# Idle transposes on TensorE in the first and in the last group of an RWKV-6 block

## The chip, the core and the metric

One core of a Trainium2 chip runs the whole kernel. The metric is the device time of one execution in microseconds (us), the median of the runs; everything is in 32-bit floats. The engines are named as in the profile: PE is TensorE (matmuls; PEld is its loading of weights), DVE is VectorE, ACT is ScalarE, POOL is GpSimd, and SP issues most of the DMA transfers.

## The reference

An RWKV-6 block: time mixing with a recurrence per head, then channel mixing. x is 32 sequences of 128 tokens and 512 channels, in 32 heads of 16.

```python
xn = ln(x);  sx = token_shift(xn, state)
xxx = tanh((xn + sx * maa_x) @ maa_w1)              # 5 x 32 columns
x5  = xn + sx * (maa_stack + xxx @ maa_w2)          # five mixed inputs
w = exp(-exp(time_decay + tanh(x5[1] @ decay_w1) @ decay_w2))
r, k, v, g = x5[3] @ Wr.T, x5[0] @ Wk.T, x5[2] @ Wv.T, silu(x5[4] @ Wg.T)
for t in range(128):                                # per head, state s is 16 x 16
    a = k_t[:, None] * v_t[None, :]
    out_t = r_t @ (u * a + s);  s = a + w_t[:, None] * s
att = groupnorm(out) * gn_w + gn_b
x = x + (att * g) @ Wo.T
xn2 = ln(x);  sx2 = token_shift(xn2, state)
rr = sigmoid((xn2 + sx2 * maa_r) @ ffn_Wr.T)
kk = relu((xn2 + sx2 * maa_k) @ ffn_Wk.T) ** 2
x = x + rr * (kk @ ffn_Wv.T)
```

## The kernel before

**Tiles and groups.** The 32 sequences are taken in 8 groups of 4. A group's activations are held channel by token: 4 blocks of 128 channels (index e) by 512 columns (4 sequences of 128 tokens). In the recurrence the 128 partitions are the 4 x 32 heads of a group.

**The streams of a group.** Each is a generator that yields its steps:

- front_mix (L422): loads x (L286); layernorm (L319): statistics on DVE (L332, L333: one pair per sequence), rstd on DVE and POOL (L350, and the power in L352), the negated mean in L354 on DVE, the normalization on ACT (L357), transposes on PE (L377, 16 per group), scale and bias on ACT (L367). Then the token shift and the first mix (L433 to L438), the matmuls with maa_w1 (L444 and, in first_split, L397), tanh, and the mix proper: matmuls L410, and per block two DVE steps (L470, L472), or from group 1 on, for three of the five inputs, DVE L465 and POOL L467. In group 0 it also calls constants() (L247), which issues the loads of the small vectors and weights and makes four small POOL products of vec (L249 to L252).
- front_proj (L492): the decay and the projections k, r and v (L391), evicted by ACT (L540) and sent through DMA to the layout of the recurrence. front_gate (L546) does the gate, which waits in DRAM.
- prep (L567): states, products of pairs and the bonus.
- the recurrence (rec_*, L670 to L776): ACT L679 and L690, POOL L704 (am) and L708 (a), DVE the scan L726 and the product L728, PE the sums L761 (transposes that accumulate), ACT the copy L775 of the sums to y. The sums lie in "acc", a PSUM tile of two banks of which there is one buffer.
- back (L784): group normalization (ACT L803 squares; DVE L806, then a Newton iteration L809 to L816, then L818), transposes L829, ACT L838, DVE L840 with the gate from a DMA (L833), matmuls with Wo L849, residual L858, the second layernorm (L357, L377, L367 again), DVE L872 and L884 and POOL for the two mixed inputs, matmuls L391 (fk), L923 (fr), L939 (fv), the output L928 and L930, and its DMA L932. For the last group, back runs as two streams of two sequences each: last1 and last2.
- center (L296) takes the mean over each head out of the weights wv, on POOL (L303 to L310), and stores them in DRAM.

**What sets the order.** Nothing runs as the generators are written down: a planner (class Plan, L73 to L179) records every step once, in one order, and the engines' queues then run it. A step names its engine, an estimate of its time, what it reads and writes, what buffers it takes and frees. The planner keeps estimated times at which each engine is free, looks at each stream's next step, and takes, among those that could start within EPSILON of the earliest, the one with the least due value (L177). DUE (L49) gives each stream its due values at its first and last step, counted in groups. So a change of EPSILON, of DUE or of a stream can move steps of others on every engine, and with them the DMAs on SP's queue.

[...] PSUM is divided by L221 into four one-bank tiles "ps" for matmul results, two "sc" for the scan and the two banks of "acc".

```python
        (ps, [P, N], "ps", 4), (ps, [P, DH, T2], "sc", 2), (ps, [P, DH, P], "acc", 1),
```

The line numbers here are those of the kernel before. In the changed one they are one higher from L239 to L946, and 15 higher in the lines that add the streams to the plan.

Of the kernel before, what the change touches and what calls it, by code (L numbers as in the profile page):

```python
# [8 lines left out]
F32 = mybir.dt.float32  # L9
# [5 lines left out]
P = 128  # L15
# [5 lines left out]
NG = B // GB  # L21
# [14 lines left out]
PE, DVE, ACT, POOL, SP = range(5)  # L36
# [6 lines left out]
LANDING = 2.0  # L43
HOP = (0.2, 0.05, 0.05, 0.04, 0.08)
ON_POOL = (2, 3, 4)
EPSILON = 0.0388


DUE = {"rec": (0.171, 1.108), "mix": (-4.67, -2.417), "proj": (-4.683, 4.311), "gate": (0.588, 0.608), "prep": (-4.19, 1.684), "back": (-0.012, 3.928), "last1": (-21.388, 9.796), "last2": (10.392, 13.665)}  # L49


class Buf:
# [20 lines left out]
class Plan:  # L73
# [103 lines left out]
    def pick(self, best):  # L177
        t0 = min(t for t, _ in best)
        return min((x for x in best if x[0] <= t0 + EPSILON), key=lambda x: x[1][3] + x[1][4] * x[1][2])  # L179


@with_exitstack
def rwkv6_block(ctx: ExitStack, tc: tile.TileContext, x, prev, s0, vecs, u, maa_w1, maa_w2,
# [11 lines left out]
    nc = tc.nc  # L195
    ctx.enter_context(tc.manual_schedule())
    const = ctx.enter_context(tc.tile_pool(name="const", bufs=1))
# [5 lines left out]
    def tag(pool, shape, name, bufs):  # L203
        def make():
            count[0] += 1
            return pool.tile(shape, F32, tag=name, bufs=bufs, name=f"{name}_{count[0]}")
        return make, bufs
# [14 lines left out]
    plan = Plan({name: tag(pool, shape, name, bufs) for pool, shape, name, bufs in spec})  # L222
# [12 lines left out]
    dw2p = const.tile([P, E // 2], F32, name="dw2p")  # L235
    thb = Buf(const.tile([P, N], F32, name="thb"))
    ident = const.tile([P, P], F32, name="ident")
    mhalf = const.tile([P, GB], F32, name="mhalf")
    by_head = const.tile([P, P], F32, name="by_head")  # L239
    make_identity(nc, ident)  # L240
# [543 lines left out]
    def back(g, d, bs=range(GB), W=None):  # L784
# [158 lines left out]
        if W is None:  # L943
            frt.open = fvt.open = False

    data = [dict() for _ in range(NG)]  # L946
    for gen, n in ((rec_dve, 2), (rec_pool, 3), (rec_act, 1), (rec_state, 1), (rec_pe, 2), (rec_out, 0.1)):
        v0, v1 = DUE["rec"]
        plan.add(gen(range(NG)), v0, NG - 1 + v1, n * NU * NG)
    for g in range(NG):  # L950
        for gen, name, n in ((front_mix, "mix", 40), (front_proj, "proj", 72), (front_gate, "gate", 17),
                             (prep, "prep", 40), (back, "back", 140)):
            v0, v1 = DUE[name]
            if name != "back" or g < NG - 1:
# [4 lines left out]
    for bs, name in (((0, 1), "last1"), ((2, 3), "last2")):  # L959
        v0, v1 = DUE[name]  # L960
        plan.add(back(NG - 1, data[-1], bs, W), NG - 1 + v0, NG - 1 + v1, 130)
    plan.run()


# [35 lines left out]
```

## Time and profile before

| | |
|---|---|
| median of 3 runs | 1533.85 us (1533.52 to 1534.64) |
| profiled execution, its own time | 1535.0 us |
| span of its instructions | 1533.2 us |
| mean granted TensorE clock | 0.959 |
| busy: PE / PEld / DVE / ACT / POOL | 1410.0 / 746.6 / 1270.9 / 656.2 / 1024.8 us |
| instructions | 16578 |
| period of a steady group | 170.26 us |
| DMA, mean over the span | 96 GB/s |

A view of instructions has, per row: start and duration in us, the engine, the line, the operation, output <- input by the program's names, the size of the stationary operand, the shape, the type and the count (x) of instructions that the row joins; in brackets, the idle time before it on its engine and what ended it. A matmul of 512 columns in 32-bit floats counts as two in the profile, a transpose as one. "PEclk", and "granted clock" in a table by stretch, is the clock that TensorE was allowed, as a share of full speed; in this trace it is 0.5 or 1.0 at any one moment. Busy tenths divide the span into 40 equal slices of 38.3 us.

### The profile page before, as it was taken

What the parts mean: (1) busy time and instruction counts of PE and PEld (TensorE: products, weight loads), DVE (VectorE), ACT (ScalarE), POOL (GpSimd) and SP (SyncE); (2) the same over time, 40 slices, a digit from 0 to 9 for tenths busy, and PEclk for the clock granted to TensorE, in tenths of its full rate; (3) what the DMA queues carried; (4) which work ended last, traced back from release to release, by engine and by line L of the source; (5) the groups of instructions that cost most, each with busy time, mean ns of one, the idle gap of its engine ahead of it and who ended that gap; (6) DMA issues with size and microseconds to landing.
All of it is one profiled execution on the core that took longest, in us unless ns stands there. A gap on an engine that the chain in (4) does not pass through costs nothing.

```text
span 1533.2 us, 16578 instructions
## 1 busy us (share of the span) xinstructions
PE 1410.0 (92%) x5344; PEld 746.6 (49%) x5344; DVE 1270.9 (83%) x1618; ACT 656.2 (43%) x1277; POOL 1024.8 (67%) x632
## 2 busy tenths in 40 slices
PE   3997898899999999999999999999999998778788
PEld 1343454455554555455554555455544555455444
DVE  5537789989998899899988899899988898878732
ACT  4233242423743356323743365424733354344242
POOL 3014893877787859687786959686777959678400
PEclk9798899899999999999999999999999999889879
DMA  6120331244304431244304521343305421400220
GB/s 223 42 84 23 104 108 29 78 132 145 117 11 144 144 131 43 79 133 142 117 29 134 183 92 35 97 140 124 110 32 163 126 89 41 159 27 28 93 71 28
DMA packets 127559, 146.88 MB, mean 96 GB/s; under 512 B 8176, under 2 KB 77296, under 8 KB 126448
## 3 DMA queue, kind: packets, MB, share of 16 engines
q1 hardware_dynamic: 92112, 128.81, 25.6%
q10 hardware_dynamic: 35360, 17.02, 3.9%
q8 instruction: 42, 0.69, 0.2%
q14 instruction: 45, 0.37, 0.1%
HBM read 94.41 MB, written 17.83 MB: 73 GB/s over the span
## 4 chain that ended last, share of the span: by engine, by line
PE 51%; DVE 27%; POOL 13%; issue 6%; DMA 2%; ACT 1%; SPq 1%; DVEq 0%; POOLq 0%; ACTq 0%
PE ps L391 18%; PE acc L761 8%; POOL am L704 7%; PE ps L939 6%; PE ps L923 6%; PE ps L410 6%; DVE sc L726 5%; POOL a L708 4%; DVE rm L728 4%; PE ps L849 2%; DVE rk L642 2%; DVE ps L634 2%; PE ps L397 2%; PE ps L444 2%; DVE ps L470 1%
## 5 line engine op out<-in xcount | busy, mean ns | idle before, releaser
L704 POOL TENSOR_TENSOR am<-v,k 128x1024 f32<-128x1024 f32 x256 | 610.3, 2384 | 88.7 <-DMA r<-blk 70.4
L391 PE MATMUL ps<-mx,wt 128*128 128x512 f32 (+1 forms) x1312 | 583.2, 593 | 8.8 <-DVE mx L472 3.4
L708 POOL TENSOR_TENSOR a<-am 128x504 f32<-128x504 f32 x256 | 286.1, 1118 | 201.5 <-DVE sc L726 181.1
L391 PEld LDWEIGHTS ps<-mx,wt 128*128 128x128 f32 x1312 | 244.3, 194 | 276.2 <-issue 259.1
L728 DVE TENSOR_TENSOR rm<-sc,r 128x1024 f32<-128x1024 f32 x256 | 312.9, 1222 | 38.3 <-PE acc L761 22.9
L726 DVE TENSOR_TENSOR_SCAN sc<-sc,a 128x512 f32<-128x512 f32 x256 | 313.4, 1224 | 32.7 <-POOL a L708 30.5
L761 PE MATMUL acc<-by_head,rm 128*128 128x128 f32 x2176 | 290.8, 283 | 36.0 <-DVE rm L728 29.9
L761 PEld LDWEIGHTS acc<-by_head,rm 128*128 128x128 f32 x2176 | 252.3, 146 | 135.9 <-issue 54.4
L679 ACT COPY sc<-w 128x512 f32<-128x512 f32 x256 | 151.4, 591 | 219.5 <-DVE rm L728 197.0
L690 ACT COPY a<-st 128x8 f32<-128x8 f32 x256 | 52.2, 204 | 180.1 <-DVE sc L726 156.4
L467 POOL TENSOR_TENSOR mx<-mx,xnT 128x512 f32<-128x512 f32 x84 | 99.7, 1198 | 40.9 <-DVE mx L465 40.3
L923 PE MATMUL ps<-wt,mx 128*128 128x512 f32 x256 | 115.7, 595 | 0.0
L540 ACT COPY blk<-ps 128x512 f32<-128x512 f32 x96 | 56.0, 584 | 137.6 <-PE ps L391 137.6
L849 PE MATMUL ps<-wt,mx 128*128 128x512 f32 x256 | 112.8, 598 | 0.6 <-DVE rk L642 0.6
L410 PE MATMUL ps<-tha,w2p 64*128 64x512 f32 x256 | 89.1, 677 | 18.0 <-DVE mx L472 12.0
L939 PE MATMUL ps<-wt,ev 128*128 128x512 f32 x224 | 102.4, 600 | 2.7 <-DVE mx L472 2.7
L352 POOL TENSOR_TENSOR rstd<-rstd,mhalf 128x4 f32<-128x4 f32 (+1 forms) x17 | 20.2, 1191 | 120.1 <-DVE rstd L350 120.1
L470 DVE SCALAR_TENSOR_TENSOR ps<-ps,vec,sx 128x512 f32<-128x512 f32 x76 | 57.3, 753 | 36.7 <-PE ps L410 36.3
L465 DVE SCALAR_TENSOR_TENSOR mx<-ps,vec,sx 128x512 f32<-128x512 f32 x84 | 61.8, 743 | 21.8 <-PE ps L410 21.7
L849 PEld LDWEIGHTS ps<-wt,mx 128*128 128x128 f32 x256 | 48.9, 192 | 62.5 <-issue 56.5
L923 PEld LDWEIGHTS ps<-wt,mx 128*128 128x128 f32 x256 | 46.4, 190 | 51.0 <-issue 46.8
L939 PEld LDWEIGHTS ps<-wt,ev 128*128 128x128 f32 x224 | 40.9, 192 | 45.3 <-issue 39.9
(108 smaller groups left out, 1341.1 us busy)
## 6 DMA issues: line engine op xcount, KB each, us to landing
x<-in_x SPq DMA_DIRECT2D x15, 1024.0 KB
wt<-in_wk SPq DMA_DIRECT2D x8, 1024.0 KB
wt<-in_wr SPq DMA_DIRECT2D x8, 1024.0 KB
wt<-in_wg SPq DMA_DIRECT2D x8, 1024.0 KB
dgate<-blk SPq DMA_DIRECT2D x32, 256.0 KB
wt<-in_wo SPq DMA_DIRECT2D x8, 1024.0 KB
wt<-in_fk SPq DMA_DIRECT2D x8, 1024.0 KB
wt<-in_fr SPq DMA_DIRECT2D x8, 1024.0 KB
```

The costliest lines, as they stand in the source:

```text
L391: nc.tensor.matmul(p, lhsT=w[:, c, e * P : (e + 1) * P], rhs=xin[:, c, cols], start=(c == 0), stop=(c == NE - 1))
L410: nc.tensor.matmul(p.t, lhsT=w[h, :], rhs=t[h, :], start=True, stop=True)
L467: nc.gpsimd.tensor_tensor(bt(x5[:, f, :]), bt(x5[:, f, :]), row(xnT, f, 1), ALU.add)
L679: nc.scalar.copy(sc.t, d["w01"][:, q : q + 1, :].to_broadcast([P, DH, T2]))
L704: nc.gpsimd.tensor_tensor(am.t, v[:, ds, :], k[:, q : q + 1, :].to_broadcast([P, DH, L]), ALU.mult)
L708: nc.gpsimd.tensor_tensor(a[:, :, 1:T2], am2[:, :, 0 : T2 - 1, 0], am2[:, :, 0 : T2 - 1, 1], ALU.add)
L726: nc.vector.tensor_tensor_scan(scf, scf, a.t.rearrange("p d n -> p (d n)"), 0.0, ALU.mult, ALU.add)
L728: nc.vector.tensor_tensor(pair(rm.t), sc.t.unsqueeze(3).to_broadcast([P, DH, T2, 2]), r2[:, q : q + 1, :, :].to_broadcast([P, DH, T2, 2]), ...
L761: nc.tensor.matmul(acc[:, i, :], lhsT=rm[:, i, :], rhs=by_head, is_transpose=True, start=(q == 0 and i % 4 == 0), stop=(q == S), skip_grou ...
L849: nc.tensor.matmul(p.t, lhsT=att[:, c, b * L : (b + 1) * L], rhs=wot[:, c, :], start=(c == 0), stop=(c == NE - 1))
L923: nc.tensor.matmul(p.t, lhsT=xr[:, c, b * L : (b + 1) * L], rhs=frt[:, c, :], start=(c == 0), stop=(c == NE - 1))
L939: nc.tensor.matmul(p2.t, lhsT=kv[:, c, b * L : (b + 1) * L], rhs=fvt[:, c, :], start=(c == 0), stop=(c == NE - 1))
```

## The change

Two streams are added, each of one generator, `warm(n, need)`: n steps of two transposes of the identity matrix into the banks of acc, and at the end a copy by ACT of one column to a new tile thw of one column, which nothing reads. The results of the transposes are used nowhere. "warm0" has 90 steps (180 transposes), is free to begin at once, and has due values around those of group 0's front; "warm1" has 60 steps (120 transposes), begins after the last sums have been copied (`"rec" in data[NG - 1]`), and is due among the last group's back. EPSILON goes from 0.0388 to 0.0457, and the due values of the other streams are set anew, last2's by the most.

```diff
-EPSILON = 0.0388
+EPSILON = 0.0457
-DUE = {"rec": (0.171, 1.108), "mix": (-4.67, -2.417), "proj": (-4.683, 4.311), "gate": (0.588, 0.608), "prep": (-4.19, 1.684), "back": (-0.012, 3.928), "last1": (-21.388, 9.796), "last2": (10.392, 13.665)}
+DUE = {"rec": (0.169, 1.075), "mix": (-5.141, -3.246), "proj": (-5.191, 5.259), "gate": (0.565, 0.599), "prep": (-4.508, 1.678), "back": (0.059, 3.118), "last1": (-21.936, 10.98), "warm0": (-5.0, -3.0), "warm1": (5.624, 7.819), "last2": (6.858, 12.052)}
...
+    thw = Buf(const.tile([P, 1], F32, name="thw"))
...
+    def warm(n, need):
+        acc = None
+        for _ in range(n):
+            if acc is None:
+                (acc,) = yield Op(PE, 0.215, w=[(0, None)], alloc=["acc"], need=need)
+            else:
+                yield Op(PE, 0.215, w=[(acc, None)])
+            for i in range(2):
+                nc.tensor.transpose(acc[:, i, :], ident, ident)
+        yield Op(ACT, 0.2, r=[(acc, None)], w=[(thw, None)], end=[acc])
+        nc.scalar.copy(thw[:, 0:1], acc[:, 0, 0:1])
...
+    for name, n, need in (("warm0", 90, None), ("warm1", 60, lambda: "rec" in data[NG - 1])):
+        v0, v1 = DUE[name]
+        plan.add(warm(n, need), (0 if name == "warm0" else NG - 1) + v0, (0 if name == "warm0" else NG - 1) + v1, n)
```

What the planner makes of it, by the two orders of instructions:

- PE, front: 110 of the 180 transposes stand before the first L377, 18, 8 and 28 behind its second, third and fourth group of four, 16 between L397 and the first L410.
- PE, end: 50 of the 120 stand behind the last L761 and before the first L829; 36 behind the first two pairs of L829; 8 among the next; then come the eight matmuls of L849 for the first half (16 in the profile's count), 8, a pair of L829, 8, a pair of L829, 10, and L849 of the second half, with four transposes L377 of the first half between its two sequences.
- SP, front: the load of wv (1 MB), which stood second, right behind x, now stands behind all constants and before wk; vec and pv follow x at once.
- DVE, front: four pairs of statistics (group 1) stand before the mix of group 0 instead of eight (groups 1 and 2); the other four are spread over the mix.
- The steady groups keep their order but for one L391 ahead of one L761, one L728 behind the first L872, and a few steps of ACT. Some more steps change places in groups 0 and 1 (130 to 340 us) and in 1290 to 1445 us.
- SP, end: the load of x for the first half and the gates of the halves come in another order.

## The prediction

> **What bounds the kernel now.** I read the page first, then the busy time in nine stretches of 170 us, then the instructions in the first 70 us and in the last 90. On the page, the busy tenths in 40 slices show where TensorE (PE) isn't full, and the clock row where it is slow; the chain says who sets the end.
>
> ```profile
> PE   3997898899999999999999999999999998778788
> ...
> PEclk9798899899999999999999999999999999889879
> ...
> PE 51%; DVE 27%; POOL 13%; issue 6%; DMA 2%; ACT 1%; SPq 1%; DVEq 0%; POOLq 0%; ACTq 0%
> ```
>
> A full clock is 9 or more in that row. It dips in the first slices and in the last seven or so; between them PE is full and the clock too. The table by stretch says the same in numbers (first, a middle, the last; columns: stretch, its length, then PE, weight loads, DVE, ACT, POOL busy, granted clock, DMA share, GB/s):
>
> ```profile
> 0.00:170.00 170.00, 123.44 (x353) 53.66 (x354) 99.89 (x151) 59.51 (x105) 49.77 (x43) 0.87 0.28 88
> 681.20:851.50 170.30, 167.89 (x666) 88.74 (x665) 156.18 (x198) 80.33 (x156) 130.02 (x79) 1.00 0.33 106
> 1362.00:1533.00 171.00, 138.21 (x499) 80.46 (x497) 97.97 (x142) 70.68 (x144) 67.72 (x42) 0.88 0.16 53
> ```
>
> So what idle work on TensorE can win lies in two places only, and the steady groups (period 170.26 us) have nothing to give.
>
> The front, on PE:
>
> ```profile
> 16.10 0.47 PE L377 MATMUL ps<-ident,x 128*128 128x128 f32 x1 [16.10 <-ACT x L357]
> ...
> 18.22 3.03 PE L377 MATMUL ps<-ident,x 128*128 128x128 f32 x13 [0.23 <-ACT x L357]
> 21.90 5.51 PE L444 MATMUL ps<-mx,w_sb 128*128 128x512 f32 x8 [0.65 <-PE ps L377]
> ```
>
> 3.03 us for 13 transposes is 0.233 each: a cold clock (warm, four take 0.60 in one row at 104.74 and their starts lie 0.11 apart). The clock column reads 1.00 here, but only because it has no change on record before 35.65; I trust the durations. Ahead of it the normalization waits for a small load, which is not a matter of the clock:
>
> ```profile
> 11.13 0.19 POOL L249 TENSOR_SCALAR ffn<-vec 128x4 f32<-128x4 f32 x1 [8.88 <-DMA vec<-in_vecs]
> ```
>
> The vectors were issued only at 6.11, when x had landed. POOL takes L249–L252 and then the power L352 (to 12.89), DVE's L354 stands beside POOL's first centering step L303 and takes 2.27 us to 15.20 (0.16 elsewhere), and ACT's L357 begins at 15.24. Later DVE waits:
>
> ```profile
> 30.18 0.69 DVE L332 BATCH_NORM_STATS2 stats<-x 128x6 f32<-128x512 f32 x1 [3.95 <-DMA x<-in_x]
> ```
>
> Eight pairs of statistics, for groups 1 and 2, keep DVE to 37.43; only then the mix of group 0 begins (37.51, L470/L472), 16 steps at 1.40 us and 3.9 us of stalls, to 63.85. The first projection follows at 62.52. The mix is the front's critical piece, not PE.
>
> The tail: the last L761 ends at 1446.55; ACT copies the sum (L775) by 1448.46, and DVE normalizes one half, then the other:
>
> ```profile
> 1455.23 1.08 PE L829 MATMUL ps<-ident,y 128*128 128x128 f32 x4 [8.69 <-DVE y L818]
> 1460.55 2.92 PE L829 MATMUL ps<-ident,y 128*128 128x128 f32 x12 [4.24 <-DVE y L818]
> 1463.52 15.16 PE L849 MATMUL ps<-wt,mx 128*128 128x512 f32 x32
> ```
>
> PE idles 8.69 and 4.24 us and comes back cold: L849 takes 15.16 where the other half, at 1345.25, took 13.75.
>
> **Do transposes warm the clock at all?** The Trainium skill's page "TensorE: Matmul & The Clock Gate", in "Part 4: PE-mode transpose", says that in one kernel the full clock doesn't engage for transpose mode, since it doesn't count as busy in the same way. That speaks straight against this change. This trace decides otherwise. From 1371.95 on PE did 24 transposes, cold, 5.2 us back to back, and the granted clock went 0.50 to 1.00 at 1377.1; the same happened at 1343.0, after 16 transposes and 8 matmuls of that size:
>
> ```profile
> 1342.50:1343.00 0.50, 0.50 (x3) 0.12 (x1) 0.50 (x2) 0.18 (x1) 0.44 (x1) 0.50 0.00 0
> 1343.00:1343.50 0.50, 0.02 (x1) 0.00 (x0) 0.50 (x1) 0.44 (x1) 0.50 (x1) 0.99 0.00 0
> ```
>
> The two changes lie 34.1 us apart. By the rows, a run of transposes costs 0.22 us each for 3.4 to 5.2 us and about 0.108 after (eight L761, same shape, take 1.04 to 1.09 warm). By the page, all 110 transposes ahead of the first L377 would cost 0.22.
>
> **The change, part by part.** The order of instructions shows three things that count; thw and its ACT copies (0.2 us, after work that is off the chain) I put at nothing: in the front ACT waits for PE there.
>
> *Vectors first.* On SP's queue the load of wv moves behind the small constants, so vec and pv follow x at once instead of after its landing. Vec should land near 6.5 instead of 11.1. L249, L352 and L354 then come 4.4 us sooner, L354 without wv's centering beside it; ACT's L357 starts near 10.8 and ends near 13.8. The price: wv's 1 MB now stands ahead of wk, in a stretch in which the DMAs are full (about 400 GB/s from 20 to 32.5), against an SP queue that is some 3.8 us further on. Group 1's x landed at 30.15; I take 27.4 (26.5 to 29).
>
> *The front's idle transposes.* 110 stand before the first L377. From about 1.4 us, 16 to 32 of them cold (3.5 to 7.0 us), the rest at 0.108 (10.1 to 8.4): they end at 15.0 to 16.8, I take 15.7. So PE, not ACT, releases the first L377: 0.4 us sooner than the 16.10 of before, and 1.9 later than x is ready. L377 then runs at 0.108; 18, 8 and 28 more stand behind its second, third and fourth four, 54 x 0.108 = 5.8 us. PE reaches L444 near 23.3 and leaves it, warm (8 x 0.43 = 3.4), at 26.8, against 27.3. Sixteen more before L410 (1.7 us): its first two banks are ready near 30.4 against 29.2 plus 2 x 0.4. DVE isn't there before 31, so it is covered; without that cover (x1 at 26.5) it costs 1 us.
>
> *DVE's order.* Only four pairs of statistics stand before the mix instead of eight. The mix then starts at 27.4 + 4 x 0.79 + 0.6, near 31.2 to 32.5 instead of 37.5: 5 to 6.3 us sooner. The four other pairs (3.2 us, with what hangs on them 3.8) are now inside the mix, partly in its 3.9 us of stalls: I take 2.5 of it paid. The mix ends 2.5 to 4 sooner, and the first projection starts near 59.0 to 60 instead of 62.52. I take 3.5 us (bounds 1.5 and 5). PE works without a gap that matters from there to 116, so the gain is carried to the start of the recurrence (131.5), if the transfers that r waits for follow. The clock during the mix isn't kept: L410 comes two at a time, 1.1 us per 1.4, as before.
>
> *The middle.* In each steady group one L391 goes ahead of one L761, one L728 behind the first L872: PE is full either way, 0 to -0.5 us a period. Some rows change places in groups 0 and 1 (130 to 340 us) and in 1290 to 1445. No row prices that; a POOL step L704 is 2.4 us, so one misplaced step each way is -3 to +3. I take 0, as the periods after it are bound by the same work.
>
> *The tail's idle transposes.* The sums have one buffer, so the 50 that stand first wait for L775, at 1448.5 (times of before): 5.4 us warm, to 1454.1, or 7 to 8 us cold. y of half 1 is ready at 1455.1, so they are hidden. Then two pairs of L829, and 36 more (3.9 us): the third pair comes near 1459.8, where before it came at about 1460.6, behind half 2's first. Half 1 ends L829 near 1461, and its L849 can start near 1462.2; warm, 16 x 0.43 = 6.9, to 1469.1 instead of 1471.8 (-2.7). But 26 more idle ones (2.8 us) and half 2's last two pairs of L829 stand behind it in the same queue, and ACT's L838 and DVE's L840 for those (1.6 us, plus the hops): half 2's L849 starts near 1473.2, has L377 of half 1 between its sequences, and ends near 1480.7 instead of 1478.5. L377 and L872 of the last half then end near 1483.6, where they did (1483.7): the 2.7 us is given back. What is left is L391 at 1486.08, where 24 short matmuls took 7.24 and would take 24 x 0.215 = 5.2 warm: 1.9 us, which I give 4 in 10, and small change. I take -0.5 (bounds -2.5 and +2.5).
>
> **The sum.** -3.5 + 0 - 0.5 = -4 us. The profiled execution took 1535.0 with a span of 1533.2, so 1531.0 for one like it; on the median of the runs, 1533.85, it is 1529.8. About 0.2% (3.1 us) is what a measurement of this kernel can tell from no change, so same means 1530.8 to 1536.9.
>
> **The rivals.** *The clock is kept warm all along*: the mix's stalls go (L410's x4 in 3.46 at 39.04 becomes half that; 2 of 3.9), the first projection isn't cold to 66.5 (2 us), and the tail keeps both its 1.4 in L849 and its 1.9 in L391. -3.5 - 4 - 3.3 = -10.8, or 1523. For it: 300 transposes are many. Against: none stand in the mix or between 1481 and 1486, where the clock is lost. Chance 0.14.
>
> *The front's gain is lost on the way*: x1 lands at 29 to 30 because wv is ahead of it, or the recurrence's start is held by the transfers to the lanes (POOL at 131.5 waits for r's), not by the projection. Then the gain is 0 to 1.5, and with the tail's -0.5 the time is near 1533. For it: the DMAs are full there, and the last waits before 131.5 are DMAs. Against: those transfers are issued behind the projections, which come sooner. Chance 0.22.
>
> *Slower: the idle transposes hold the real ones in PE's queue at the end.* If the burst at 1448.5 starts cold, 50 take 7.2 to 8 us and end at 1456; the 36 end at 1461; with 26 more, half 2's L849 ends at 1482 to 1483, 3.5 to 4.5 later than before, and all behind it is one chain (PE without a gap from 1486 to 1528). With a front gain of 0 to 1, or a loss in the changed order of groups 0 and 1, that is near 1537.5. It decides once half 2's L849 ends after about 1482 on the old scale. Chance 0.16.
>
> *It doesn't do what it says* (the page's rule holds): 110 x 0.22 end at 25.6, 54 more and 16 L377 cold add 15.6, L444 starts at 41 instead of 21.9, and the mix near 53.5: 16 us later, 1550. The rows at 1377.1 exclude it nearly. Chance 0.03.
>
> That leaves 0.45 for the forecast, with a range of its own of 1526.5 to 1532. The range, 1521 to 1538, leaves out the last rival and the edges. Faster by over 0.2%: most of 0.45, and 0.14, some of the second rival, 0.55; within 0.2%: 0.25; slower: 0.20.
>
> **What would show it.** L957's starts 0.22 apart for 3.4 to 7 us and then 0.108; L358 on ACT (L357 before) at 10.8; the first L378 near 15.7; the mix's first step at 31 to 32.5; the first L392 near 59 to 60; the period still 170.26. In the tail L850's first half 15.6 us after the last L762, its second ending some 34 us after. I'm wrong if the mix starts after 34, if the period moves, or if the last half's L850 ends over 1 us from that.

## The result, and the profile after

The changed kernel takes 1521.8 us (4 runs, 1519.66 to 1525.66), against 1533.81 before: ratio 0.9924 [0.9902, 0.9945]. A later set of runs beside the experiments gave 0.9906 [0.9891, 0.9921]. It is 12 us faster; forecast was 4, with a range from 1521 to 1538 us. The profiled execution took 1520.89 us, span 1519.1 (before 1535.0 and 1533.2), so the two traces differ by 14.1 us. The same three rows of the page, after:

```profile
PE   8997999899999999999999999999999999778998
...
PEclk9798999899999999999999999999999999889999
...
PE 50%; DVE 23%; POOL 14%; issue 6%; ACT 4%; DMA 2%; SPq 1%; ACTq 0%; POOLq 0%; DVEq 0%
```

PE now looks full from the first slice, but that is the idle work itself. The clock row gains at the end. The stretches say it in numbers (columns as before):

```profile
0.00:170.00 170.00, 147.33 (x549) 75.59 (x550) 97.33 (x153) 60.08 (x106) 51.06 (x43) 0.86 0.30 97
680.00:850.30 170.30, 167.81 (x665) 88.69 (x664) 156.12 (x198) 80.66 (x156) 129.81 (x79) 1.00 0.32 106
1348.00:1519.00 171.00, 147.94 (x630) 93.86 (x628) 102.51 (x144) 71.70 (x147) 71.08 (x44) 0.95 0.16 55
```

In the first stretch PE is busy 24 us more. The clock column seems no better there (0.86 after 0.87), but it reads 1.00 until the first change on record. In the clock records of the traces that first change, to full, comes at 25.46 us before (not at 35.65, as the prediction has it) and at 4.24 us after; with half speed up to there the two are about 0.79 and 0.85. In the last stretch the clock went from 0.88 to 0.95. In the steady part it is full in both. Now the front, instructions of PE and then the two waits of POOL and DVE:

```profile
1.34 13.62 PE L957 MATMUL acc<-ident 128*128 128x128 f32 x110 [1.34 <-POOL ident masks.py:199]
14.80 1.04 PE L378 MATMUL ps<-ident,x 128*128 128x128 f32 x8
...
22.44 3.60 PE L445 MATMUL ps<-mx,w_sb 128*128 128x512 f32 x8
...
60.05 10.34 PE L392 MATMUL ps<-mx,wt 128*128 128x512 f32 x17
```

```profile
6.65 0.19 POOL L250 TENSOR_SCALAR ffn<-vec 128x4 f32<-128x4 f32 x1 [4.39 <-DMA vec<-in_vecs]
```

```profile
30.91 0.69 DVE L333 BATCH_NORM_STATS2 stats<-x 128x6 f32<-128x512 f32 x1 [7.96 <-DMA x<-in_x]
```

110 transposes in 13.62 us are some 15 cold ones and the rest at 0.108: transposes do warm the clock. vec came 4.5 us sooner. But x of group 1 still landed near 30.9, so DVE's wait, where all those gains ran to, is 7.96 us instead of 3.95. The mix starts at 34.31 instead of 37.51 only because four pairs of statistics stand ahead of it and not eight. The end:

```profile
1437.35 7.35 PE L957 MATMUL acc<-ident 128*128 128x128 f32 x50 [1.96 <-ACT y L776]
...
1450.88 7.03 PE L850 MATMUL ps<-wt,mx 128*128 128x512 f32 x16
...
1464.89 3.60 PE L850 MATMUL ps<-wt,mx 128*128 128x512 f32 x8
...
1473.79 5.42 PE L392 MATMUL ps<-mx,wt 128*128 128x256 f32 x24 [1.58 <-DVE mx L885]
```

The burst starts cold; L850 is warm, and so are the 24 short matmuls at 1473.79, which took 7.24 before:

```profile
1486.08 7.24 PE L391 MATMUL ps<-mx,wt 128*128 128x256 f32 x24 [1.07 <-DVE mx L884]
```

Lining up the same instruction in both traces shows where the 14.1 us came from (start in us; scans are counted from 0):

| | before | after | difference |
|---|---|---|---|
| first projection (L391 / L392) | 62.52 | 60.05 | -2.5 |
| POOL's first product (L704 / L705) | 109.16 | 108.31 | -0.9 |
| first scan (L726 / L727) | 130.30 | 131.34 | +1.0 |
| scan 24 | 267.98 | 261.22 | -6.8 |
| scan 40 | 345.28 | 338.90 | -6.4 |
| scan 44 | 368.06 | 358.18 | -9.9 |
| scan 208 | 1247.46 | 1238.75 | -8.7 |
| last scan | 1436.72 | 1426.60 | -10.1 |
| last copy of the sums (L775 / L776) | 1446.58 | 1435.43 | -11.2 |
| last L930 / L931 | 1529.41 | 1515.30 | -14.1 |

The front's 2.5 us were gone by the first scan. More than half of the gain arises between 131 and 268 us, where no idle transpose stands; between scans 44 and 208, in the steady groups, 1.2 us are lost again. So there were two theories. A: the new order of the steps brings most of it. B: the clock that the transposes keep brings it.

### The profile page after: what moved, and what is told of

Its sections match the earlier page's. It is cut to its first block, busy times and chain, and to the rows that moved or that the text cites. A ratio compares the mean times of both kernels' runs of the same rounds, so it can differ in the third digit from the quotient of the medians.

```text
span 1519.1 us, 17193 instructions
## 1 busy us (share of the span) xinstructions
PE 1433.7 (94%) x5644; PEld 775.6 (51%) x5644; DVE 1266.1 (83%) x1618; ACT 657.3 (43%) x1279; POOL 1026.1 (68%) x632
## 4 chain that ended last, share of the span: by engine, by line
PE 50%; DVE 23%; POOL 14%; issue 6%; ACT 4%; DMA 2%; SPq 1%; ACTq 0%; POOLq 0%; DVEq 0%
PE ps L392 17%; POOL am L705 8%; PE acc L762 8%; PE ps L940 6%; PE ps L924 6%; PE ps L411 6%; POOL a L709 5%; DVE sc L727 4%; DVE rm L729 3%; PE ps L850 2%; PE ps L445 2%; DVE ps L635 2%; DMA x<-in_x 2%; PE ps L398 1%; DVE rk L643 1%
## 5 line engine op out<-in xcount | busy, mean ns | idle before, releaser
L705 POOL TENSOR_TENSOR am<-v,k 128x1024 f32<-128x1024 f32 x256 | 610.9, 2386 | 71.1 <-DMA r<-blk 52.7
L392 PE MATMUL ps<-mx,wt 128*128 128x512 f32 (+1 forms) x1312 | 581.3, 591 | 7.7 <-DVE mx L885 3.1
L392 PEld LDWEIGHTS ps<-mx,wt 128*128 128x128 f32 x1312 | 242.6, 193 | 273.7 <-issue 261.7
L727 DVE TENSOR_TENSOR_SCAN sc<-sc,a 128x512 f32<-128x512 f32 x256 | 313.4, 1224 | 31.5 <-POOL a L709 28.7
L850 PE MATMUL ps<-wt,mx 128*128 128x512 f32 x256 | 111.7, 592 | 0.2 <-DVE rk L643 0.2
L850 PEld LDWEIGHTS ps<-wt,mx 128*128 128x128 f32 x256 | 48.2, 190 | 59.8 <-issue 55.0
```

The costliest lines, as they stand in the source:

```text
L392: nc.tensor.matmul(p, lhsT=w[:, c, e * P : (e + 1) * P], rhs=xin[:, c, cols], start=(c == 0), stop=(c == NE - 1))
L705: nc.gpsimd.tensor_tensor(am.t, v[:, ds, :], k[:, q : q + 1, :].to_broadcast([P, DH, L]), ALU.mult)
L727: nc.vector.tensor_tensor_scan(scf, scf, a.t.rearrange("p d n -> p (d n)"), 0.0, ALU.mult, ALU.add)
L850: nc.tensor.matmul(p.t, lhsT=att[:, c, b * L : (b + 1) * L], rhs=wot[:, c, :], start=(c == 0), stop=(c == NE - 1))
```

## Experiments 1 to 3: the order without the transposes

In the changed kernel the planner still counts the steps of warm, so that all others keep their places, but the transposes and ACT's copy aren't issued (`if False`, or for one stream alone):

```diff
-            for i in range(2):
+            for i in range(2 if False else 0):            # order_none
+            for i in range(2 if n == 90 else 0):          # order_front: warm0 alone
+            for i in range(2 if n == 60 else 0):          # order_tail: warm1 alone
                 nc.tensor.transpose(acc[:, i, :], ident, ident)
```

> The changed kernel with all 300 idle transposes and both copies left out, the planner still counting them: every other instruction stands where the change put it. Theory A (the new order of steps brings most, 9 of the 12 us; the transposes bring only the tail's 3): 1524 to 1526 us. Theory B (the clock that the transposes keep brings most): 1531 us or more. Either way the clock is cold until about 25 us in the front, L850 of the first half begins cold at the end.

> The changed kernel with the 120 idle transposes of the tail left out, those of the front in place, order unchanged. Theory A: as the kernel without any, 1524 to 1526 us. Theory B: the front's share of the clock is kept, so some 6 to 9 us faster than without any; the tail lacks 3 us of the change's gain: about 1525.

> The changed kernel with the 180 idle transposes of the front left out, those of the tail in place, order unchanged. Theory A: within 1 us of the changed kernel, 1521 to 1523 us. Theory B: 6 to 9 us slower than the changed kernel, 1528 to 1531 us.

Measured: without any, 1521.14 us, ratio 0.9915 [0.9901, 0.9928]; warm0 alone 1521.01, 0.9909 [0.9896, 0.9923]; warm1 alone 1519.08, 0.9899 [0.9884, 0.9914]. The changed kernel again, in the last set:

> The changed kernel itself, on the chip and in the rounds of the others, for a narrower interval than its first four runs gave. If the idle transposes bring nothing on balance: within 1.5 us of the order alone (ratio to before 0.990 to 0.993). If they bring the 3 us that the tail seemed to gain: ratio 0.988 to 0.990.

1521.15 us, 0.9906 [0.9891, 0.9921]. All four intervals overlap: as far as these runs can tell, **the whole gain is there without a single idle transpose**, and theory B falls. Even A was too modest: all three kernels came out faster than the ranges it gave, and the order alone brought 13 us, not 9.

The traces show what the transposes do inside that. In the front, the first projection starts at 58.72 and 59.32 in the two kernels without warm0, at 59.17 with warm0 alone, at 60.05 and 60.39 in the two profiles of the change: warm0 brings nothing here, and may cost up to 1.7 us. In the tail, from the last copy of the sums to the last output, the kernel without any gains 0.3 us on before, the one with warm1 3.0. Here is the order alone, PE, at the end:

```profile
1447.73 9.21 PE L850 MATMUL ps<-wt,mx 128*128 128x512 f32 x16
...
1471.83 7.11 PE L392 MATMUL ps<-mx,wt 128*128 128x256 f32 x24 [1.59 <-DVE mx L885]
```

L850 of the first half is cold (9.21 for 7.03 warm) and the 24 short ones too (7.11 for 5.42). So warm1 can buy 2.6 us on top of the order, and warm0 may give some of that back; what is left of the sum is below what these runs tell apart.

## Experiment 4: the load of wv

```diff
-        nc.sync.dma_start(out=t.t, in_=ap if after else ap.rearrange("(c p) o -> p c o", p=P))
+        load = lambda: nc.sync.dma_start(out=t.t, in_=ap if after else ap.rearrange("(c p) o -> p c o", p=P))
+        if ap is wv and not held:
+            held.append(load)
+        else:
+            load()
...
+        held[0]()                                         # the last line of constants()
```

> The kernel before with one edit: the load of wv is issued behind the constants instead of right behind x; all other instructions keep their order. vec lands near 6.5, L357 starts near 11. Theory A: the early part of the gain alone, 1 to 3 us, as DVE still has eight pairs of statistics before the mix: 1531 to 1533 us. Theory B: no change, 1533 to 1534 us.

1534.83 us, ratio 1.000 [0.9992, 1.0008]. The first L377 starts at 12.15 instead of 16.10 and L444 at 17.95, yet the mix starts at 37.44 (37.51 before):

```profile
30.11 0.69 DVE L339 BATCH_NORM_STATS2 stats<-x 128x6 f32<-128x512 f32 x1 [7.82 <-DMA x<-in_x]
...
37.44 0.75 DVE L477 SCALAR_TENSOR_TENSOR ps<-ps,vec,sx 128x512 f32<-128x512 f32 x1
```

Four microseconds of an earlier start end in a longer wait for the same DMA. vec's wait was real and worth nothing.

## Experiments 5 to 9: which part of the order

The planner's picks of both kernels were written down as lists of streams, and a kernel without warm replays a list, so that the order of one kernel can be used in one stretch and the other's in the rest:

```diff
-            best = []
-            for st in self.streams:
+            for n, name in enumerate(self.order):         # the first of the list that can start
+                st = next(x for x in self.streams if x[5] == name)
                 t = self.start(st[1])
                 if t is not None:
-                    best.append((t, st))
-            assert best, "no stream can go on"
-            t, st = self.pick(best)
+                    break
+                assert n < 400, "no stream can go on"
+            del self.order[n]
```

In the traces, each engine has before's order outside the stretch that was replaced. Theory C: each stretch has a gain of its own. Theory D: the front's lead is what the middle makes use of.

> No idle transposes. Every step ahead of the first product of the recurrence (POOL, about 109 us) in the order of the changed kernel (wv behind the constants, four pairs of statistics before the mix), every later step in the order of before. Theory C (each stretch of the order has its own gain, as the profile of the order alone shows it): the first projection 3.7 us sooner, the start of the scan 1.8 us sooner, 1531 to 1532 us. Theory D (the front's lead is what the middle turns into 9 us): 1524 to 1527 us.

> No idle transposes. The order of before, but from the first product of the recurrence (about 109 us) to about 256 us that of the changed kernel. Theory C: the middle's own gain, 5.5 to 8 us: 1526 to 1528 us. Theory D: next to nothing, 1532 to 1534 us.

> No idle transposes. The order of before, but from the first product of the recurrence (about 109 us) to about 184 us that of the changed kernel. If the middle's gain is DVE's chain at the start of the recurrence (before, L647 took 2.72 us at 147.19 beside POOL's L704, 0.7 elsewhere, and the bonus stands ahead of the scans), about 3 us of the 8: 1530 to 1532 us. If it is the order at the end of the first group (190 to 256 us), next to nothing: 1533 to 1535 us.

> No idle transposes. The order of before, but from about 260 to 480 us that of the changed kernel. Theory C: 2.4 us, seen near the 44th scan (368 us): 1531 to 1532 us. Theory D: nothing, 1533 to 1534 us.

> No idle transposes. The order of before to about 1190 us, from there that of the changed kernel, with the order of the last half's back. Theory C: 1 to 3 us between 1276 and 1350 us, as much again gained and given back in the tail: 1531 to 1533 us. Theory D: 1533 to 1534 us.

| order of the changed kernel in | us | ratio to before | in its own stretch of the trace |
|---|---|---|---|
| front, to 109 us | 1530.64 | 0.9971 [0.9964, 0.9979] | -2.4, kept to the end |
| 109 to 256 us | 1526.26 | 0.9947 [0.9933, 0.9961] | +0.7 at POOL's first product, -5.5 at scan 24: -6.1 |
| 109 to 184 us | 1530.48 | 0.9962 [0.9950, 0.9975] | +2.1 at POOL's first product, -2.4 at scan 24: -4.5 |
| 260 to 480 us | 1534.59 | 1.0003 [0.9995, 1.0011] | 0 |
| from 1190 us | 1530.98 | 0.9976 [0.9970, 0.9983] | -2.0 at scan 208, -5.3 at the end: -3.3 |

C holds: the middle has its gain without the front's lead, so D falls. C missed in one place: 260 to 480 us gave nothing, where the table above has 3.5 us between scans 40 and 44.

**The middle's own gain.** Three quarters of it come before 184 us. DVE sets the pace there. Before, in its first scans:

```profile
145.40 0.67 DVE L647 TENSOR_TENSOR blk<-r,k 128x512 f32<-128x512 f32 x1
146.10 1.05 DVE L650 TENSOR_REDUCE a<-blk 128x64 f32<-128x512 f32 x1
147.19 2.72 DVE L647 TENSOR_TENSOR blk<-r,k 128x512 f32<-128x512 f32 x1
...
152.34 1.22 DVE L726 TENSOR_TENSOR_SCAN sc<-sc,a 128x512 f32<-128x512 f32 x1
```

and POOL beside it:

```profile
147.03 2.34 POOL L704 TENSOR_TENSOR am<-v,k 128x1024 f32<-128x1024 f32 x1
```

L647 began 0.16 us behind L704 and ended after it. In the changed order the same step comes at 146.68, beside L705 of 144.49 to 146.85, and takes 0.72:

```profile
146.68 0.72 DVE L648 TENSOR_TENSOR blk<-r,k 128x512 f32<-128x512 f32 x1
...
149.84 1.22 DVE L727 TENSOR_TENSOR_SCAN sc<-sc,a 128x512 f32<-128x512 f32 x1
```

That is 2.0 us. The bonus pairs (L634 and L642, 2.2 us each) also stand one place earlier, so that one lies ahead of the first scan instead of behind the second, which is why the first scan starts 1.0 us later and the fifth 2.5 sooner; by the fifth scan this has evened out. So 2.0 of the 4.5 us are there at the fifth scan, and the other 2.4 come between it and scan 24. There DVE waits less for PE's L410. The longest of these waits before, and the same one with the order of 109 to 184 us replaced:

```profile
176.56 0.75 DVE L465 SCALAR_TENSOR_TENSOR mx<-ps,vec,sx 128x512 f32<-128x512 f32 x1 [2.83 <-PE ps L410]
```

```profile
172.09 0.75 DVE L505 SCALAR_TENSOR_TENSOR mx<-ps,vec,sx 128x512 f32<-128x512 f32 x1 [1.54 <-PE ps L450]
```

Shortly ahead of it the clock of before is at half (0.50 from 168.8 to 172.2 us, PE busy all the while), and that of the spliced kernel is full (1.00 from 160.5 to 184 us). All six profiles with before's order in this stretch lose the clock there for 3.4 us, none of the other eight does. So part of the order's gain is a clock that it keeps, without any idle transpose; how much, and the 1.6 us from 184 to 256, I did not take apart.

**The 3.5 us at scan 44 come without a change of order.** The kernel with the late splice has before's instructions in before's order on every engine up to 1252 us, and has the gain all the same. Clock and PE of before, then of the late splice, by windows of 3.4 us:

```profile
329.40:332.80 3.40, 2.75 (x9) 1.16 (x10) 3.40 (x4) 0.74 (x3) 3.40 (x4) 0.98 0.54 225
332.80:336.20 3.40, 3.40 (x15) 2.91 (x14) 3.11 (x4) 1.37 (x4) 3.40 (x3) 0.52 0.25 71
```

```profile
330.60:334.00 3.40, 2.75 (x10) 1.17 (x11) 3.40 (x5) 0.75 (x3) 3.40 (x4) 1.00 0.53 222
334.00:337.40 3.40, 3.40 (x19) 2.20 (x18) 3.10 (x4) 1.35 (x4) 3.40 (x3) 1.00 0.25 68
```

PE is busy 2.75 of 3.4 us in both, with the same gaps; in one the clock goes to 0.5 for one window, in the other not. PE then is 1.7 us late (its L829 at 347.74 is 2.46 us behind scan 40, 0.77 in the other), DVE's bonus slips from the end of a POOL step to the start of one, and waits for it. DVE and POOL of before:

```profile
353.00 2.32 DVE L634 TENSOR_TENSOR ps<-r,k 128x512 f32<-128x512 f32 x1
...
360.97 1.74 DVE L634 TENSOR_TENSOR ps<-r,k 128x512 f32<-128x512 f32 x1
```

```profile
352.40 2.36 POOL L704 TENSOR_TENSOR am<-v,k 128x1024 f32<-128x1024 f32 x1
...
359.80 2.35 POOL L704 TENSOR_TENSOR am<-v,k 128x1024 f32<-128x1024 f32 x1
```

and of the late splice:

```profile
353.22 0.87 DVE L674 TENSOR_TENSOR ps<-r,k 128x512 f32<-128x512 f32 x1
...
359.74 0.67 DVE L674 TENSOR_TENSOR ps<-r,k 128x512 f32<-128x512 f32 x1
```

In the 14 profiles at hand it is one to one: six lost the clock in that window, and take 22.8 us from scan 40 to 44; eight did not, and take 19.3 or 20.4. Before is among the six and both profiles of the change among the eight, so the 14.1 us between the two traces hold 3.5 us of this. Which it is goes with where the clock's steps fall. The clock changes in a trace lie whole multiples of 3.41 us apart (before: 281.46, 295.11, 332.66, 336.07), on a grid that stands differently against the instructions in each trace. Counted from scan 40, modulo 3.41 us, it stands at 0.8 to 1.1 us in the six that lost the clock, and at 0.3 to 0.4 or 1.6 to 3.3 us in the eight that kept it. Chance alone may not set it: of the six profiles with before's order from 109 to 184 us five lost the clock, of the eight with the changed order one. So the changed order may make the loss rarer, and the runs with 109 to 256 us replaced, 8 to 9 us faster than before where their stretch shows 6.1, point the same way. With one or two profiles of each kernel that isn't shown; nor is it that this is why executions of one kernel here differ by 3 to 6 us.

The gains in the profiles' own stretches, -2.4, -6.1, 0 and -3.3, come to -11.8; with scan 44's -2.4 in the profile of the order alone, that is -14.2, and its trace has -14.4. By the ratios of the runs the four come to about 15.8 us, more than the order alone's 13.0, a difference that their intervals together allow. What makes the late 3.3 I did not take apart.

## Experiments 10 and 11: transposes in other places

The transposes alone, in the order of before (the 36 came to stand behind the third pair of L829, which waits for half 2's L818, so the tail isn't quite the change's):

```diff
+            if g == 0 and sums is None and e == 0:
+                idle(110)                                 # then 18, 8, 28, and 16 ahead of L410
...
+                if bs == (0, 1) and e == 0:
+                    idle(50)
+                if bs == (0, 1) and e == 2:
+                    idle(36)
```

> The order of before in every instruction, with idle transposes alone added: 110, 18, 8, 28 and 16 in the front as in the changed kernel, 50 ahead of the first L829 of the last group and 36 behind its third pair. If the transposes themselves bring nothing in the front (DVE waits for x of group 1 either way) and only a warm L849 at the end: 1532 to 1535 us, L849's 32 in 13.8 us instead of 15.2. If the clock they keep is what the gain is made of: 1524 to 1528 us.

1539.25 us, ratio 1.0025 [1.0015, 1.0036]: slower. L444 starts 5.4 us later, the mix only 0.35, and 0.4 us stays to the tail: the front's transposes are covered by the wait for x, and bring nothing. In the tail L849 starts 5.7 us later, behind the 36, which run cold in 6.48 us; it is warm (14.00 for 15.16), as are the short matmuls. The last output comes 3.2 us later. Neither forecast held; in the tail the loss is that of the place where I put the 36.

And transposes where the clock was really lost, in the mix of group 0:

```diff
                 side_by_side(pp, w2p[:, m, i * P : (i + 1) * P], up, low)
+                if g == 0 and (m, i) != (1, 0):
+                    idle(40 if (m, i) == (1, 1) else 12)
```

> The changed kernel without the front's 180 idle transposes, but with 40 behind the first two pairs of L410 of group 0 and 12 behind each later pair, where PE waits for DVE's mix; the tail's 120 in place. If the clock is worth something there: it stays full from about 25 us to the first projection, which is no longer cold for its first 4 us: 2 us faster than without them, 1516 to 1518 us. If DVE's mix sets the pace and 12 transposes delay a pair: 0 to 3 us slower, 1519 to 1522 us.

1520.2 us, ratio 0.9901 [0.9885, 0.9916], against 0.9899 without them: no difference. The clock did as intended: in the first 62 us it is 0.94, against 0.82 in the kernel without them.

```profile
0.00:62.00 62.00, 45.50 (x212) 26.38 (x213) 39.48 (x73) 24.96 (x40) 14.61 (x22) 0.94 0.47 156
```

```profile
0.00:62.00 62.00, 39.65 (x99) 15.69 (x100) 39.75 (x74) 26.11 (x41) 14.62 (x22) 0.82 0.47 156
```

The first projection starts 1.4 us later (each 12 stand ahead of a pair that DVE waits for) and then runs warm, so that POOL's first product comes 1.1 us sooner. A full clock through the whole mix is worth 1 us by this one profile, which lost more than that at scan 44 and in the tail's short matmuls, which fell cold (8.23 us). No version tried is clearly faster than the changed kernel; warm1 alone, at 1519.08, is the lowest, with an interval that overlaps.

## Why the prediction was right, and where it was wrong

- *Transposes warm the clock*: right. Some 15 cold ones, then 0.108: 110 in 13.62 us, where the rule that spoke against it, of the Trainium skill's page "TensorE: Matmul & The Clock Gate" in "Part 4: PE-mode transpose", would make it 24.2 (110 times the cold 0.22). The rule doesn't hold in these traces, and the last rival is out. The first L378 came at 14.80 (forecast 15.7).
- *Vectors first*: vec at 6.65 and L358 at 11.04 as forecast (6.5 and 10.8). The step "Group 1's x landed at 30.15; I take 27.4" was wrong: 30.9. With wv alone moved it landed at 30.1 too. The second rival's "29 to 30" was nearer.
- *DVE's order*: the right cause of the front's gain, and the only one left, as the load of wv brings nothing alone (experiment 4); no run has DVE's order alone. The mix started at 34.31, not 31.2 to 32.5 and later than the 34 that I had named as a sign of being wrong, but the other four pairs cost only 0.7 us within it, not the 2.5 I charged: the first projection at 60.05, forecast "59.0 to 60".
- *"so the gain is carried to the start of the recurrence (131.5)"*: right for the order of the front (2.5 us carried to the first scan in its splice), not for the profile after. From the first projection to POOL's first product it took 48.3 us against 46.6; the granted clock between 79 and 88 us was 0.62 against 0.81 before and with the order alone (half speed twice as long), which goes with part of it. From there to the first scan it took 23.0 us against 21.1, with the bonus ahead of that scan.
- *The middle*: this is the step that failed. "No row prices that; a POOL step L704 is 2.4 us, so one misplaced step each way is -3 to +3. I take 0, as the periods after it are bound by the same work." The start of the recurrence isn't bound by the same work as the periods: DVE's chain is, and it had rows to price it. L647 at 2.72 beside 0.67 stood in the trace of before. Measured -6.1, outside the -3 to +3, and -3.3 for the late reordering, its tail included. The period, which I had at 170.26 or up to 0.5 less, is 170.4 after: a second sign of being wrong that came.
- *The tail*: L850 started 15.45 us after the copy of the sums (forecast 15.6) and the second half's ended 33.1 after it (34). The 24 short matmuls stayed warm, the case I gave 4 in 10: 3.0 us gained in all, 0.5 forecast. That is the term that was mis-sized: 1.8 us from those, 1.1 from a shorter way to them. The rival in PE's queue at the end didn't come about.
- The likeliest case lay at 1529.8, with a range of its own of 1526.5 to 1532, and the time at 1521.8, which I had given to the rival of a clock kept warm all along (1523). The number was that rival's, the cause was not. That the whole range holds the time, by 0.8 us, is luck: it reached down to 1521 for that rival, and what filled it was the middle, which I had put at 0.

## What to carry to other kernels

If an order is made by a planner, a change that adds idle work and tunes the planner anew is two changes; issue the new order without the new instructions before crediting them. Price each reordering where one engine's chain is tight, by asking which of its instructions are longer there than elsewhere. Work that shortens a path ahead of a wait for a DMA only makes the wait longer: find what ends the wait first.

## What the runs showed of the hardware

- A DVE step with two inputs in SBUF waits for a POOL step that is already under way: of the 32 steps L634, 14 took 1.0 us or more instead of 0.70, and each of those 14 began with 0.45 us or more of a POOL step L704 still to run; L647 once took 2.72, L354 once 2.27 for 0.16. Where L634 began together with POOL's L708, at 700.06 us, it took 0.69 and L708 was the longer, 1.57 for 1.03. L472, L726 and L728, with an input in PSUM, never did (76 and twice 256 of them). The Trainium skill's page "SBUF — State Buffer", in "🔬 SBUF: two separate sides", says so: the pair of ports is held for the whole instruction by the one that comes first. The traces agree.
- The same instructions with the same gaps lose the clock in one execution and keep it in another (the windows at 332.8 and 334.0). The same skill's page "TensorE: Matmul & The Clock Gate", in "Part 1: The HAM clock gate", has a window that runs freely and varies from run to run; what these traces add is that one such window, 3.4 us at half speed, cost 2.4 to 3.5 us behind it, by shifting DVE's bonus onto a POOL step, and nearly all of that was still there at scan 208.
